# A decoder layer on one core: keys rotated by a permutation, low-rank products in two row slots, and a newly planned order

## The chip, the cores and the metric

The kernel runs on one core of a Trainium2 chip. A core has five engines with queues of their own: TensorE (PE in the profile; PEld is its weight load) multiplies matrices into PSUM, VectorE (DVE), ScalarE (ACT) and GpSimd (POOL) work on elements, and SyncE (SP) issues the transfers between DRAM and the on-chip memory SBUF. Each queue runs its instructions in the order in which they were written; semaphores hold an instruction back until its inputs are there. The time is device microseconds of one execution, from launch to end.

## What is computed

The layer works on x of shape (2 batches, 512 tokens, 1024 features), in three steps, each of which adds its result to x.

```python
x = x + attn(layernorm(x))      # 32 heads of 32 in 8 groups; weights sign(w) times a scale per row
x = x + xattn(layernorm(x))     # 256-wide reads, 16 heads of 16 with rotary positions and a causal mask,
                                # a state update, a gated product with ctx, a second state update
x = x + ffn(layernorm(x))       # x @ kernel + bias + low-rank terms picked by gate, and shared ones
```

Two lines of it are what the change touches. In the second step the keys (and queries) are rotated by position:

```python
x1, x2 = (x[..., :half], x[..., half:])
return jnp.concatenate([x1 * cos - x2 * sin, x2 * cos + x1 * sin], axis=-1)
```

In the third step the term of rank 32 is added to the dense product: `delta_flat = einsum('bor,btr->bto', B_eff, Ax)` with `Ax = einsum('bri,bti->btr', A_eff, x)`; batch rows are taken in eight groups of 128 tokens, each with factors of its own.

## The kernel before, in words

Tokens lie in tiles of 128, four per batch. The stages carry names that appear in the profile's tile names. `proj0` and `proj1` make q, k and v of the first attention (activations split in three bf16 parts). `maxA` and `maxB` compute the scores of batch 0 and batch 1 once and reduce them to row maxima; `attA` and `attB` compute them again, exponentiate and multiply by v. `outA` and `outB` are the output projections, `factor` makes the low-rank factors. `stateA` and `stateB` read the state, project and rotate q and k of the second attention; `maxC`, `attC`, `maxD`, `attD` are its maxima and attention; `tailA` and `tailB` are the state updates and the gated product; `weights`, `denseA` and `denseB` are the last step.

**Maxima.** `peaks` (L550) walks over groups of four heads. Per query tile, `scores` (L200) issues four matmuls with 32 contracted rows, one in each of the four 32-row slots of the array, into two pairs of PSUM banks; `reduced` (L581) takes maxima of each pair on VectorE (two reductions of 128x1024). When a group is done, `turned` (L588) splits the negated maxima into three bf16 parts, transposes them on TensorE, and copies them to a `shift` row. In the attention three rows of `shift` times a constant of ones (`ones16`) are added to the scores by a small matmul, which subtracts the maximum.

**Attention.** `attend` (L614) goes over groups and four key tiles: score matmuls, exponentials on ScalarE, value matmuls; `added` (L661) adds up the probabilities on VectorE, `finished` (L669) sums them over partitions on TensorE, and the result is scaled and split into three bf16 parts, partly on GpSimd. `direct` with `SPARE` decides whether the last key tile is added on VectorE or summed by extra matmuls.

**Rotation.** `rotations` (L865) computes sines and cosines of all positions (small instructions on VectorE, two table functions on ScalarE); `rotation_table` (L950) spreads them. `state_inputs` (L1105) first reads and normalises the four tiles of a batch (`tile_of`), keeping two numbers per token in `norm` for the tails. Then it projects: `kind` 0 gives queries, 1 gives keys, 2 gives keys with the two halves of each head exchanged, from a third weight matrix `proj[2]`. `rotated` (L1143) multiplies each bank by its row of the table and, for kind 2, adds the product to the key.

**Dense step.** `dense` normalises and transposes a tile, makes its 32 ranks (`bank` with four partial sums, then a matmul with `eye` that adds them into the 32 rows of `slot`), and multiplies: for each half of 512 columns eight matmuls of 128x512 with the weights and one of 32 rows with the low-rank factor `be`. `factors_back` loads the factors from DRAM.

**What sets the order.** The instruction order is written by a planner in the kernel's own Python code, not by the program's nesting. Every stage is a generator, a job, that yields (engine, estimated time, ready time) before it emits instructions. `run` (L449) keeps a clock per engine and always advances the job whose next step can start earliest, plus the job's lag; the lags are the numbers in the job list in `build` and in `LAGS`. `clocked` slows PE steps in the plan when PE had little to do in windows of 3.41 us. `take` and `give` keep count of tiles and PSUM banks: there are two single banks (`bank`), three double ones (`pair`), eight `page`, eleven `row` and four `probs` buffers. All instructions are pinned to the planned order on each engine, so estimates and lags decide the order, and the real waits decide the time.

Of the kernel before, what the change touches and what calls it, by code (L numbers as in the profile page):

```python
# [12 lines left out]
BF16 = mybir.dt.bfloat16  # L13
I32 = mybir.dt.int32
AF = mybir.ActivationFunctionType
ALU = mybir.AluOpType
# [53 lines left out]
class Kernel:  # L70
# [79 lines left out]
    def constants(self):  # L150
# [7 lines left out]
        self.ones16 = self.const([P, P], "ones16", BF16)  # L158
        nc.gpsimd.memset(self.ones16, 1.0)
# [19 lines left out]
        )  # L179
        self.eps = self.const([P, 1], "eps")  # L180
# [5 lines left out]
        )  # L186

# [234 lines left out]
    def output_weights(self):  # L422
# [7 lines left out]
        "added": 0.0, "ahead": 0.0, "attA.ahead": -0.1, "attA.exponentials": -0.1, "attA.finished": 0.3,  # L430
        "attB.added": 0.0, "attB.ahead": -0.3, "co.emptied": -0.1, "cv.emptied": -0.1, "denseA.summed": -0.6,
        "denseB.emptied": 0.3, "denseB.summed": -2.0, "emptied": -0.6, "exponentials": 0.3,
        "factor.put": -1.0, "finished": 0.0, "gained": -1.0, "gated": -1.0, "joined": -0.6, "k.scale_of": 0.0,
        "maxA.reduced": 0.0, "maxA.turned": -0.1, "maxB.reduced": 0.3, "maxB.turned": -0.3,
        "maxD.turned": -0.3, "outA.clean": 1.0, "outA.stored": 2.0, "outB.stored": -1.0,
        "proj0.featured": -1.0, "proj0.valued": -0.6, "proj1.featured": -1.0, "proj1.valued": -0.6,
        "q.scale_of": 0.0, "residual": 1.0, "rotated": 0.0, "stateA.emptied": -0.3, "stateA.rotated": -0.1,
        "stateB.gained": 0.0, "stateB.rotated": 0.0, "stored": 0.6, "summed": -0.6, "tableB.emptied": -2.0,
        "tailA.gained": -1.0, "tailA.residual": -2.0, "tailB.gated": -0.3, "tailB.residual": 0.0,
        "v.scale_of": 0.0, "wo.scale_of": 0.0,  # L440
    }
    SPARE = 3
# [145 lines left out]
    def turned(self, name, b, g, mx, reduced, earlier):  # L588
# [3 lines left out]
        t = yield "DVE", 1.2, t  # L592
# [3 lines left out]
        nc.vector.tensor_scalar(parts[:, :, :, 0], mx, -1.0, None, ALU.mult)  # L596
        nc.vector.scalar_tensor_tensor(rest, mx, -1.0, parts[:, :, :, 0], ALU.mult, ALU.subtract)
        nc.vector.tensor_copy(parts[:, :, :, 1], rest)
        nc.vector.tensor_tensor(parts[:, :, :, 2], rest, parts[:, :, :, 1], ALU.subtract)
# [14 lines left out]
    def attend(self, groups, operands, scale, causal):  # L614
# [10 lines left out]
        def exponentials(p, s, q0, t):  # L625
# [4 lines left out]
            if causal:  # L630

                done = yield "POOL", 1.0, done
                nc.gpsimd.affine_select(
                    out=p[:, :, q0 : q0 + P], in_=p[:, :, q0 : q0 + P], compare_op=ALU.is_ge, fill=0.0,
                    base=0, pattern=[[0, 4], [1, P]], channel_multiplier=-1,
                )
            return done

        def probabilities(g, kt):
# [10 lines left out]
            for j in range(4):  # L650
                r = slice(32 * j, 32 * j + 3)
                self.mm(
                    s[j // 2][:, j % 2, q0:], lhsT=self.ones16[r, :], rhs=shift[r, q0:], start=False, stop=True
# [110 lines left out]
    def attend_1(self, b, peaks):  # L764
# [6 lines left out]
        def operands(g):  # L771
# [8 lines left out]
            def dst(av, inv, t):  # L780
# [4 lines left out]
                t = yield "POOL", 1.2, t  # L785
# [6 lines left out]
                t = yield "POOL", 1.6, t  # L792
                nc.gpsimd.tensor_copy(d[1], rest)
                t = yield "POOL", 1.9, t
# [199 lines left out]

    def read(self, x, t, w, gb, nout, dst, wide):
# [59 lines left out]
        t = yield "DVE", 0.42 * nout, t  # L1055
        for o in range(nout):
            nc.vector.tensor_scalar(
                rows[o], rows[o], mv[:, o, 0:1], rstd[:, o : o + 1], ALU.subtract, ALU.mult
            )
# [30 lines left out]
    def state_weights(self):  # L1090
# [7 lines left out]
        self.proj = [w[0][:, 0], w[0][:, 1], w[1][:, 0]]  # L1098
        self.values = w[1][:, 1].rearrange("p a b -> p (a b)")[:, :512].rearrange("p (a b) -> p a b", a=2)
        for kind in range(3):  # L1100
# [4 lines left out]
    def state_inputs(self, b, wide):  # L1105
# [10 lines left out]
        def tile_of(q):  # L1116
# [5 lines left out]
            t = yield "DVE", 1.3, t  # L1122
            nc.vector.tensor_scalar(x, x, mv[:, 0, 0:1], r, ALU.subtract, ALU.mult)
            keep = self.small([P, 2], "norm", bufs=8)
            nc.vector.tensor_copy(keep[:, 1:2], r)
            nc.vector.tensor_scalar(keep[:, 0:1], mv[:, 0, 0:1], r, -1.0, ALU.mult, ALU.mult)
# [14 lines left out]
        firsts = {}  # L1141

        def rotated(bank, kind, g, dst, t):  # L1143
            if dst is None:
# [671 lines left out]
```

## Time and profile before

| what | value |
|---|---|
| median of three runs | 1138.42 us (1137.93 to 1139.0) |
| the profiled execution's own time | 1135.51 us |
| its span, first to last instruction | 1133.8 us |
| mean granted clock of TensorE | 0.965 |
| busy PE, DVE, ACT, POOL | 1063.1, 841.2, 442.8, 239.2 us |
| moved by DMA | 70.51 MB, mean 62 GB/s |

The span lies between the first and last instruction; the execution's own time includes what lies around it. In a profile line of the timeline the first number is the start in us from the span's beginning, the second the duration, then engine, code line, operation, output and inputs, and the count; in square brackets stands the idle time of that engine before it, with what ended it. In a line of groups the numbers after the first bar are the busy time of all and the mean nanoseconds of one, after the second bar the idle time. Line numbers are mostly those of helpers (L130 is the helper for matmuls, L133 that for transposes, L51 that for the pinned engine calls), so tile names tell more. A float32 matmul with 512 columns shows as two records.

The stages follow each other so: projections and maxima A to about 215 us, attA to 302, maxB with outA and factor to 431, attB to 535, outB with stateA to 612, maxC with stateB and attC to 725, maxD, attD and tailA to 870, tails and dense tiles to the end.

### The profile page before, as it was taken

What the parts mean: (1) busy time and instruction counts of PE and PEld (TensorE: products, weight loads), DVE (VectorE), ACT (ScalarE), POOL (GpSimd) and SP (SyncE); (2) the same over time, 40 slices, a digit from 0 to 9 for tenths busy, and PEclk for the clock granted to TensorE, in tenths of its full rate; (3) what the DMA queues carried; (4) which work ended last, traced back from release to release, by engine and by line L of the source; (5) the groups of instructions that cost most, each with busy time, mean ns of one, the idle gap of its engine ahead of it and who ended that gap; (6) DMA issues with size and microseconds to landing.
All of it is one profiled execution on the core that took longest, in us unless ns stands there. A gap on an engine that the chain in (4) does not pass through costs nothing.

```text
span 1133.8 us, 16121 instructions
## 1 busy us (share of the span) xinstructions
PE 1063.1 (94%) x6364; PEld 521.5 (46%) x6364; DVE 841.2 (74%) x1390; ACT 442.8 (39%) x711; POOL 239.2 (21%) x249
## 2 busy tenths in 40 slices
PE   4889999999999998999999899989988899999998
PEld 3554353333233632332555543545465465665643
DVE  7978888578878865887777961599668677788572
ACT  6762101388500215786221255224743232332310
POOL 3442333322222303454451012001200000000000
PEclk9999999999998997999999889979998999999999
DMA  6621000101214221240113000410151001011110
GB/s 256 203 82 28 20 10 20 29 20 29 61 33 177 95 64 39 61 168 1 38 56 116 8 11 16 172 38 1 57 197 68 33 20 55 11 48 38 38 37 38
DMA packets 24784, 70.51 MB, mean 62 GB/s; under 512 B 5234, under 2 KB 5252, under 8 KB 23684
## 3 DMA queue, kind: packets, MB, share of 16 engines
q1 hardware_dynamic: 24708, 69.48, 17.9%
q8 instruction: 50, 0.82, 0.3%
q14 instruction: 26, 0.21, 0.1%
HBM read 50.59 MB, written 10.49 MB: 54 GB/s over the span
## 4 chain that ended last, share of the span: by engine, by line
PE 79%; DVE 11%; ACT 5%; issue 2%; DMA 1%; POOL 1%; SPq 0%; ACTq 0%; DVEq 0%; POOLq 0%
PE proj_bank L130 8%; PE denseA_pair L130 6%; PE denseB_pair L130 6%; PE attA_pair L130 4%; PE outA_bank L130 4%; PE attB_pair L130 4%; PE tailB_bank L130 3%; PE attB_bank L130 3%; PE attA_bank L130 3%; PE maxB_pair L130 3%; PE maxA_pair L130 3%; PE tailA_bank L130 3%; PE outB_bank L130 3%; PE stateB_bank L130 3%; PE tailB_pair L130 3%; PE tailA_pair L130 3%
## 5 line engine op out<-in xcount | busy, mean ns | idle before, releaser
L51 DVE TENSOR_REDUCE maxB_mx<-maxB_pair 128x2 f32<-128x1024 f32 x64 | 75.3, 1217 | 21.7 <-PE maxB_pair L130 21.3
L51 DVE TENSOR_REDUCE maxA_mx<-maxA_pair 128x2 f32<-128x1024 f32 x64 | 75.5, 1216 | 14.0 <-PE maxA_pair L130 14.0
L130 PEld LDWEIGHTS <-start_slab 128*128 128x128 bf16 x480 | 44.7, 98 | 68.8 <-issue 21.1
L51 DVE TENSOR_TENSOR attB_probs<-attB_probs,attB_probs 128x1024 f32<-128x1024 f32 x46 | 62.6, 1401 | 13.8 <-PE attB_bank L130 13.5
L51 ACT ACTIVATE attB_probs<-attB_pair 128x1024 f32<-128x1024 f32 x64 | 62.6, 1023 | 20.9 <-PE attB_pair L130 10.8
L51 DVE TENSOR_TENSOR attA_probs<-attA_probs,attA_probs 128x1024 f32<-128x1024 f32 x46 | 56.6, 1282 | 16.9 <-PE attA_bank L130 8.5
L51 ACT ACTIVATE attA_probs<-attA_pair 128x1024 f32<-128x1024 f32 x64 | 62.1, 1021 | 9.7 <-PE attA_pair L130 9.4
L130 PE MATMUL proj_bank<-in_slab,start_slab 128*128 128x512 bf16 x240 | 55.5, 379 | 1.7 <-ACT in_slab L51 1.7
L130 PE MATMUL proj_bank<-in_probs,start_slab 128*128 128x512 bf16 x240 | 54.7, 380 | 0.0
L130 PE MATMUL maxB_pair<-maxB_row,proj_slab 32*128 32x512 f32 x256 | 47.4, 687 | 3.1 <-DVE maxB_mx L51 3.1
L51 POOL TENSOR_SCALAR proj_row<-proj_row 128x512 f32<-128x512 f32 x24 | 47.7, 1987 | 1.9
L130 PE MATMUL outA_bank<-wo_slab,attA_slab 128*128 128x512 bf16 x192 | 46.7, 392 | 0.7 <-ACT maxB_shift L51 0.7
L130 PE MATMUL attB_pair<-proj_slab,attB_row 32*128 32x512 f32 x256 | 46.7, 685 | 0.0
L51 ACT ACTIVATE proj_row<-proj_bank,cs 128x512 f32<-128x512 f32 x20 | 13.7, 686 | 80.8 <-PE proj_bank L130 60.2
L130 PE MATMUL outB_bank<-wo_slab,attB_slab 128*128 128x512 bf16 x192 | 43.3, 379 | 0.3 <-POOL attB_slab L51 0.3
L130 PE MATMUL attA_pair<-proj_slab,attA_row 32*128 32x512 f32 x256 | 41.6, 639 | 0.3 <-ACT attA_probs L51 0.3
L51 POOL MEMSET tailB_row<- 9x128 f32 x8 | 1.6, 195 | 186.4 <-PE tailB_bank L133 70.7
L130 PE MATMUL attB_bank<-attB_probs,proj_slab 128*32 128x512 f32 x256 | 38.4, 633 | 1.1 <-DVE tableA_slab L51 0.7
L51 ACT COPY maxB_shift<-maxB_bank 128x512 bf16<-128x512 bf16 x8 | 4.7, 586 | 84.7 <-PE maxB_bank L133 84.7
L51 POOL TENSOR_SCALAR proj_slab<-proj_row 128x512 f32<-128x512 f32 x24 | 14.9, 621 | 106.6 <-ACT proj_row L51 89.0
L130 PE MATMUL maxA_pair<-maxA_row,proj_slab 32*128 32x512 f32 x256 | 36.8, 640 | 0.0
L51 POOL TENSOR_SCALAR_AFFINE_SELECT attD_probs<-attD_probs 128x512 f32<-128x512 f32 x16 | 12.1, 754 | 113.8 <-ACT attD_probs L51 104.3
(410 smaller groups left out, 2321.8 us busy)
## 6 DMA issues: line engine op xcount, KB each, us to landing
in_page<-in_x_dram SPq DMA_DIRECT2D x8, 512.0 KB, 4.1
q_page<-in_q_weight_dram SPq DMA_DIRECT2D x8, 512.0 KB, 5.3
wo_page<-in_o_weight_dram SPq DMA_DIRECT2D x8, 512.0 KB, 3.4
tailW_slab<-in_write_dram SPq DMA_DIRECT2D x3, 752.0 KB, 7.1
maxA_row<-proj_slab SPq DMA_DIRECT2D x32, 64.0 KB, 2.0
attA_row<-proj_slab SPq DMA_DIRECT2D x32, 64.0 KB, 2.0
maxB_row<-proj_slab SPq DMA_DIRECT2D x32, 64.0 KB, 2.0
outA_page<-in_x_dram SPq DMA_DIRECT2D x4, 512.0 KB, 3.7
```

The costliest lines, as they stand in the source:

```text
L51: return self.kernel.pin(getattr(self.engine, name)(*args, **kw))
L130: self.pin(self.nc.tensor.matmul(*args, **kw))
```

## The change

In `state_inputs` the third projection goes. Keys are projected first: `keyed` copies the raw bank to a row on ScalarE, multiplies the bank by the cosine row of the table, multiplies the raw row by a constant permutation matrix `swap` on TensorE, multiplies that product by the sine row and adds. Queries come after the keys. One transfer of weights fewer is issued.

In `dense` the low-rank products of both column halves stand together behind all sixteen weight matmuls. The ranks are spread by `eyes`, 64 columns wide, into two neighbouring row slots; the factor of the second half is loaded into the neighbouring slot (five transfers instead of two large ones' second), so the two products use different row slots.

`turned` splits the plain maxima, and `minus16` holds -1 where `ones16` held 1. The two `norm` instructions move from VectorE to GpSimd. Estimates of some steps, many lags, needs and `SPARE` are different, and so the planned order is.

In the planned order of PE three places differ by more than a few instructions. The opening of `maxB` has seven score tiles before the first outA matmul, where there were four. Its closing has eighteen outA matmuls between the last score tile and the transposes of its maxima, and six more behind those, where there were none. At the end the last three dense tiles come after the last tail; the last two of them are interleaved, where there was one after the other and the last tail had one dense tile behind it in PE's queue before its own. On VectorE the arithmetic of `rotations` stands in `attA` behind the second group, where it was in the middle of `factor`.

```diff
-        self.ones16 = self.const([P, P], "ones16", BF16)
-        nc.gpsimd.memset(self.ones16, 1.0)
+        self.minus16 = self.const([P, P], "minus16", BF16)
+        nc.gpsimd.memset(self.minus16, -1.0)
+        self.swap = self.const([P, P], "swap")
+        halves = [t.rearrange("p (e h i) -> p e h i", h=2, i=8) for t in (self.swap, self.ident)]
+        for h in range(2):
+            nc.vector.tensor_copy(halves[0][:, :, h, :], halves[1][:, :, 1 - h, :])
+        self.eyes = self.const([P, 64], "eyes")
+        for h in range(2):
+            nc.vector.tensor_copy(self.eyes[:, 32 * h : 32 * h + 32], self.eye)
...
-    SPARE = 3
+    SPARE = 100
...
-        t = yield "DVE", 1.2, t
+        t = yield "DVE", 0.95, t
-        nc.vector.tensor_scalar(parts[:, :, :, 0], mx, -1.0, None, ALU.mult)
-        nc.vector.scalar_tensor_tensor(rest, mx, -1.0, parts[:, :, :, 0], ALU.mult, ALU.subtract)
+        e.tensor_copy(parts[:, :, :, 0], mx)
+        e.tensor_tensor(rest, mx, parts[:, :, :, 0], ALU.subtract)
...
-        self.proj = [w[0][:, 0], w[0][:, 1], w[1][:, 0]]
+        self.proj = [w[0][:, 0], w[0][:, 1]]
...
-            nc.vector.tensor_copy(keep[:, 1:2], r)
-            nc.vector.tensor_scalar(keep[:, 0:1], mv[:, 0, 0:1], r, -1.0, ALU.mult, ALU.mult)
+            yield "POOL", 0.4, t
+            nc.gpsimd.tensor_copy(keep[:, 1:2], r)
+            nc.gpsimd.tensor_scalar(keep[:, 0:1], mv[:, 0, 0:1], r, -1.0, ALU.mult, ALU.mult)
...
-            if dst is None:
-                t = yield "DVE", 0.69, t
-                nc.vector.tensor_tensor(kk[:, g, :], kk[:, g, :], to, ALU.add)
-                self.give("row", t)
...
+        def keyed(bank, g, t):
+            tr = max(t, (yield from self.take("row")))
+            tr = yield "ACT", 0.59, tr
+            raw = self.row([P, S])
+            nc.scalar.copy(raw, bank)
+            t = yield "DVE", 0.69, t
+            nc.vector.tensor_tensor(kk[:, g, :], bank, table[:, 1, :], ALU.mult)
+            self.give("bank", max(t, tr))
+            room = yield from self.take("bank")
+            tr = yield "PE", 0.97, max(tr, room)
+            other = self.bank([P, S])
+            self.mm(other, lhsT=self.swap, rhs=raw, start=True, stop=True)
+            t = yield "DVE", 1.38, max(t, tr)
+            nc.vector.tensor_tensor(raw, other, table[:, 2, :], ALU.mult)
+            self.give("bank", t)
+            nc.vector.tensor_tensor(kk[:, g, :], kk[:, g, :], raw, ALU.add)
...
-        for kind, (y, dst) in enumerate(((ys[0], qq), (ys[1], kk), (ys[1], None))):
+        for kind, y in ((1, ys[1]), (0, ys[0])):
...
+        for j in range(4):
+            t = yield from self.fetch(
+                self.be[32 * (j ^ 1) : 32 * (j ^ 1) + 32, :, 512:], src[32 * j : 32 * j + 32, :, 512:], 128, ready
+            )
...
-        slot = slice(32 * q, 32 * q + 32)
+        slots = [slice(32 * j, 32 * j + 32) for j in (q, q ^ 1)]
+        both = slice(64 * (q // 2), 64 * (q // 2) + 64)
...
-            self.mm(bank[slot, :], lhsT=self.eye, rhs=ax[:, 0, :], start=True, stop=True)
+            self.mm(bank[both, :], lhsT=self.eyes, rhs=ax[:, 0, :], start=True, stop=True)
...
-            if h == 0:
-                ready = max(t, (yield from self.join(ranks)))
-            t = yield "PE", 1.1, ready
-            self.mm(pair[:, h, :], lhsT=ax[slot, 1, :], rhs=self.be[slot, b, cols], start=False, stop=True)
+        t = yield "PE", 0.65, max(t, (yield from self.join(ranks)))
+        for h in range(2):
+            self.mm(
+                pair[:, h, :], lhsT=ax[slots[h], 1, :], rhs=self.be[slots[h], b, h * 512 : (h + 1) * 512],
+                start=False, stop=True,
+            )
...
-                ("rot", self.rotations(), 1.5, "attA.2"),
-                ("attA", self.attend_1(0, "maxA"), 0.0, "maxA.0"),
+                ("rot", self.rotations(), 1.0, "attA.2"),
+                ("attA", self.attend_1(0, "maxA"), 0.2, "proj1"),
...
-                ("attC", self.attend_2(0, "maxC"), 0.2, "maxC.0"),
+                ("attC", self.attend_2(0, "maxC"), 0.5, "maxC"),
```

Further hunks change estimates of steps (GpSimd steps of the attention from 1.0, 1.2, 1.6 and 1.9 to 0.75, 0.75, 1.0 and 1.35) and entries of `LAGS`.

## The prediction

> **What bounds the kernel now.** I read the page first: the busy row, the slices, and the shares of the chain of waits.
>
> ```profile
> PE 1063.1 (94%) x6364; PEld 521.5 (46%) x6364; DVE 841.2 (74%) x1390; ACT 442.8 (39%) x711; POOL 239.2 (21%) x249
> PE   4889999999999998999999899989988899999998
> PEclk9999999999998997999999889979998999999999
> PE 79%; DVE 11%; ACT 5%; issue 2%; DMA 1%; POOL 1%; SPq 0%; ACTq 0%; DVEq 0%; POOLq 0%
> ```
>
> TensorE (PE) is busy 1063.1 of 1133.8 us and is 79% of the chain, so a matmul taken out shortens the run unless VectorE (DVE) bounds that stretch. The dips in the clock row are the second thing to watch: a slowed matmul counts as busy too.
>
> The groups of matmuls, with shapes kept apart, price the two products that the change touches (a float32 matmul shows as two records, so x48 is 24 matmuls and x16 is eight):
>
> ```profile
> L130 PE MATMUL stateB_bank<-stateB_probs,stateW_slab 128*128 128x512 f32 x48 | 22.5, 605 | 0.0
> L130 PE MATMUL stateA_bank<-stateA_probs,stateW_slab 128*128 128x512 f32 x48 | 21.3, 596 | 1.1 <-ACT stateB_page L51 0.7 <-DVE stateA_slab L51 0.4
> L130 PE MATMUL denseB_pair<-factorsB_slab,denseB_row 32*128 32x512 f32 x16 | 9.0, 640 | 0.0
> L130 PE MATMUL denseA_pair<-factorsB_slab,denseA_row 32*128 32x512 f32 x16 | 8.9, 633 | 0.0
> ```
>
> The timeline shows what such products take when they follow one another: the last dense tile, a score tile of the second batch with output projection behind it, and the keys of the first batch.
>
> ```profile
> 419.50 1.14 PE L130 MATMUL maxB_pair<-maxB_row,proj_slab 32*128 32x512 f32 x8
> 420.57 2.76 PE L130 MATMUL outA_bank<-wo_slab,attA_slab 128*128 128x512 bf16 x12
> 599.00 12.28 PE L130 MATMUL stateA_bank<-stateA_probs,stateW_slab 128*128 128x512 f32 x28 [0.45 <-DVE stateA_slab L51]
> 1119.83 1.12 PE L130 MATMUL denseA_pair<-factorsB_slab,denseA_row 32*128 32x512 f32 x2
> 1120.88 7.13 PE L130 MATMUL denseA_pair<-weights_slab,denseA_page 128*128 128x512 f32 x16
> ```
>
> Fourteen full matmuls take 12.28 us, 0.88 each. One low-rank matmul alone takes 1.05 from its start to the next start (1119.83 to 1120.88); four matmuls of the same shape in four row slots take 1.07 together (419.50 to 420.57).
>
> Last, the stall between the maxima of batch 1 and its attention, as windows (PE, PEld, DVE, ACT, POOL busy, then granted clock) and in the timeline:
>
> ```profile
> 427.00:431.00 4.00, 0.72 (x8) 0.53 (x11) 3.86 (x8) 0.07 (x1) 0.00 (x0) 0.79 0.00 0
> 431.00:442.00 11.00, 11.00 (x48) 2.93 (x52) 3.52 (x4) 5.09 (x6) 8.62 (x16) 0.50 0.22 73
> 442.00:450.00 8.00, 8.00 (x68) 2.40 (x60) 6.69 (x6) 6.26 (x8) 0.00 (x0) 0.94 0.14 35
> ...
> 430.28 0.61 PE L133 MATMUL maxB_bank<-ident,parts 128*128 128x128 bf16 x4 [3.41 <-DVE parts L51]
> ```
>
> One pause of 3.41 us is followed by 11 us at half clock, with PE the bound: it costs 3.4 + 5.5 = 8.9 us.
>
> **The change, part by part.** The sum is made against the profiled execution (span 1133.8, its own time 1135.51); the median of the three runs, 1138.42, lies 2.9 above it, and I carry the differences over to the median.
>
> *Rotated keys.* Per batch the third projection goes: 4 groups x 2 matmuls. Four products with the constant `swap` come, of the same form. Net 4 matmuls of 0.88 per batch, 8 in all: -7.0 us. The vector work is the same, 12 instructions of 0.69 per batch for keys and queries. New are four copies of a bank on ScalarE (0.59 each, as the bank copies of attA), and ScalarE is busy only 1.9 of 21 us between 591 and 612. The chain of one key is longer (copy 0.6, product 0.9, multiply 0.7, add 0.7), and there are only two banks, so the danger is that PE waits for a bank. In the planned order of batch 0 the projection of the next group (1.75) lies between a projection and its swap product, longer than multiply or copy (0.7 each); followed by hand, one wait of half a microsecond stays, before the second query. Keys first, queries last, so the queries cover the last key. Ends: -7.0, and 0 if every one of the 8 swaps waits 0.9. I take -7.0: PE has no idle time in those 12.28 us and the cover is there in the order.
>
> *Low-rank products.* Per tile, two matmuls of 1.05 each at separate places become two in neighbouring row slots, into the two halves of a pair. The nearest row is four in four slots at 1.07, so I take 1.07 for the two: 1.03 saved per tile, 8 tiles, -8.3 us. Ends: 0 if the two do not overlap, -8.4 if they cost what one does. The spreading product with `eyes` has 64 output rows in place of 32 (0.38 us now, bounded by the 0.27 of a 128-wide transpose on one side and by 0.6 on the other: within +-2 us over 8, taken as 0). The ranks are needed 16 matmuls later instead of 8, which loosens a wait.
>
> *Small edits.* `swap` and `eyes`: four copies on DVE at the start, of 0.4 us or less by the copy of `spread` there, inside 2.85 us in which DVE waits for the first page. The maxima split without the sign: four instructions of 0.2 us as before. `norm` moves two instructions (0.15 and 0.20 us) per tile from DVE to POOL, eight times: at most 2.8 us of DVE, hidden by PE; behind them in POOL's queue stands the cleaning of outB, which waits if the statistics are late, but POOL is free half of the time there. One 512 KB load fewer with the state weights; the back-load of the second factor is five transfers instead of one, some 1.7 us more of SP's queue at about 0.4 us an issue, ahead of weights that land 14.4 us after issue; 0, at worst +2. The limit on direct sums (3 to 100) does nothing: 46 additions each in attA and attB is already the most that 8 groups give.
>
> *The order.* Most of the order is the same. Three places differ enough to price.
> (a) Closing of the batch-1 maxima. Before, the last score tiles stand together and PE waits for the last reduction. After, 18 outA matmuls (0.23 each, 4.1 us) stand between the last score tile and its transposes; the reductions (2.35) and the split (0.9) take 3.3. The pause goes, and with it the half clock: -8.9; ends -3.4 (clock falls for another reason) and -8.9.
> The Trainium skill ("TensorE: Matmul & The Clock Gate", Part 1) says that the clock returns to full after one busy window of about 3.4 us; as an estimate from that page the half clock would cost 1.7 us here and this term would be -5.1. The row shows 11 us at 0.50, so the row decides.
> (b) Opening of the same maxima, around 303 to 318. Before, outA starts at 309.9 after four score tiles; after, seven stand ahead of it in PE's queue. Three tiles are 3 x 2.35 us of reductions, plus a split (0.85) and one attA subtraction (0.7): outA starts 8.6 us later, of which PE fills 3 x 1.07 + 0.4 = 3.6. +5.0. The three tiles are not lost, the later bunch at 350 to 366 is one tile shorter; against that stands more half clock. Ends 0 and +10.
> (c) The 7 us of angle arithmetic (DVE, 383.7 to 390.7, hidden there: PE never pauses) now stand in attA. There a group takes 10.5 us and DVE works 8.85 of them, so the adds of one group come 7 - 1.7 = 5.3 us late; the sums that need them have 2 us of slack (adds end near 240.1, the sums start at 242.2). +3; ends 0 and +7.
> At the end the last tail is now covered by three dense tiles instead of one, and the 3 us between the last two tiles (1109.8 to 1112.8, transposes, ranks) lie beside another tile: -2; ends 0 and -3.
>
> Sum: -7.0 - 8.3 - 8.9 + 5 + 3 - 2 = -18.2. Against the median: 1138.4 - 18.2 = 1120.2, about 1120 us. What comes next where the stall of (a) is gone: attB at full clock, 97% of PE from there.
>
> **The rivals.**
> 1. *The pair does not overlap.* For it: no row shows two slots alone, and the records of the scores do not say how four share the time. Against: 1.07 for four leaves no room for serial work. It gives 1138.4 - 18.2 + 8.3 = 1128.5.
> 2. *The new order gives back what it wins.* (b) and (c) at their upper ends (+10, +7) and (a) at its lower (-3.4): -7.0 - 8.3 - 3.4 + 17 - 2 = -3.7, so 1134.7. For it: both places are bound by DVE, whose share is 72 of 99 us in attA and 12.6 of 13 between 297 and 310.
> 3. *Slower: the closing stage stalls on DVE.* The last tail write now has three dense tiles behind it, about 55 us of PE, so all eight tails' vector work must be done some 20 us earlier. Between 875 and 1094 DVE is busy 160 of 219 us; squeezed into 200 it is 80%, with PE in order behind it. The price is that of the pause at 427: 8.9 us each. From the third such pause on (26.7 against 18.2) the kernel is slower; three give 1147, the second leaves about even, 1138.
> 4. *More pauses vanish.* Windows at 0.7 of the clock also stand at 736 to 760 and 865 to 884, and two such pauses fewer give 1138.4 - 18.2 - 10 = about 1110. For it: less PE work moves every later window; against: the order there is nearly unchanged, and the maxima of batch 1 of the second attention are bound by DVE (22.2 of 24 us).
>
> **How the numbers follow.** Forecast, 1113 to 1126: 0.55. Rival 1 (1126 to 1132): 0.12. Rival 2 (1132 to 1136): 0.12. Rival 3 (over 1136): 0.10. Rival 4 (under 1113): 0.11. A measurement here tells about 0.2% (2.3 us) from no change. Of rival 3 the two-pause case (0.02) and of rival 2 its very end (0.01) are no change, 0.03; the rest of rival 3 is slower, 0.08; faster is what remains, 0.89. The range leaves out rival 3 and the lower half of rival 4: 1109 to 1135; it is wide because (b), (c) and the closing stage are priced by hand. The forecast's own range is 1113 to 1126.
>
> **What the profile after would show.** stateA_bank and stateB_bank with `stateW` as weights: x32 instead of x48, and x8 with `swap` in all four per batch at 0.88 each; ScalarE copies of 0.59 beside them. The low-rank rows start-to-next 1.07 for x4 records, not 2.1. No pause before the last maxB_bank and a clock near 1.00 from 430 on; outA starting about 318 with PE idle around it; attA some 3 us longer with the sums waiting for attA_probs. PE busy near 1043, idle still about 70. Wrong would make it: x4 records that take 2 us, PE waiting for DVE for over 3 us at a time after 875, or half clock at a place that has none now.

## The result and the profile after

The changed kernel takes 1151.68 us in the median (1148.56 to 1154.89) against 1138.18 beside it; the ratio on record is 1.0139, 95% interval 1.0116 to 1.0162 (the two medians alone divide to 1.0119). It is slower by 1.4%, where 1.6% faster was forecast. Run once more on another chip (`f3_after` below) it gave 1.0106, 1.0087 to 1.0126. The profiled execution took 1154.89 us, the longest of its four (span 1153.2, granted clock 0.943, against 0.965 before). All times below come from executions at a mean clock of 0.94 or more; the profiled execution of `f2_mid` ran at 0.556 and took 1701.07 us, so it and its trace are left out.

The page, busy row and slices:

```profile
PE 1068.6 (93%) x6316; PEld 529.7 (46%) x6348; DVE 840.1 (73%) x1380; ACT 446.5 (39%) x717; POOL 243.3 (21%) x265
PE   5889999989999999999999889999988899998998
PEclk9999999989978999999999689969998899998999
```

PE has 48 records fewer (the second profile of the same program has 6348, so 16 fewer are the change's and 32 are missing from this trace), and yet is busy 5.5 us longer; it is idle 84.6 us instead of 70.7. The clock row dips in places where it did not before. The groups of matmuls show that the operations themselves became cheaper, as planned:

```profile
L130 PE MATMUL stateB_bank<-stateB_probs,stateW_slab 128*128 128x512 f32 x32 | 15.8, 615 | 0.4 <-DVE stateB_slab L51 0.4
L130 PE MATMUL stateA_bank<-stateA_probs,stateW_slab 128*128 128x512 f32 x32 | 14.6, 599 | 0.0
L130 PE MATMUL stateB_bank<-stateB_row,swap 128*128 128x512 f32 x8 | 4.5, 644 | 1.7 <-DVE stateB_slab L51 1.6
L130 PE MATMUL stateA_bank<-stateA_row,swap 128*128 128x512 f32 x8 | 4.3, 618 | 0.7 <-DVE stateA_slab L51 0.7
L130 PE MATMUL denseA_pair<-factorsB_slab,denseA_row 32*128 32x512 f32 x16 | 4.9, 633 | 0.0
L130 PE MATMUL denseB_pair<-factorsB_slab,denseB_row 32*128 32x512 f32 x16 | 4.5, 640 | 0.0
```

The low-rank rows fell from 17.9 to 9.4 us, the projections with their swaps from 43.8 to 39.2. Against these 13 us saved stand slower matmuls and pauses. The timeline of PE shows the pauses (the number in brackets) where the kernel before had none, or shorter ones: 4.04 at the maxima of batch 0 of the second attention (1.26 before), 5.34 ahead of the first dense tile (2.82 before).

```profile
254.23 1.23 PE L130 MATMUL attA_pair<-proj_slab,attA_row 32*128 32x512 f32 x3 [3.65 <-ACT attA_probs L51]
664.78 0.58 PE L133 MATMUL maxC_bank<-ident,parts 128*128 128x128 bf16 x4 [4.04 <-ACT stateB_probs L51]
785.11 0.61 PE L133 MATMUL maxD_bank<-ident,parts 128*128 128x128 bf16 x4 [1.38 <-DVE parts L51]
832.65 0.92 PE L133 MATMUL tailA_bank<-ident,tailA_row 128*128 128x128 f32 x4 [1.35 <-DVE tailA_row L51]
864.36 0.38 PE L133 MATMUL tailA_bank<-ident,tailA_few 128*8 128x128 f32 x1 [2.52 <-ACT tailA_row L51]
894.28 1.11 PE L133 MATMUL denseA_bank<-ident,denseA_page 128*128 128x128 f32 x4 [5.34 <-DVE denseA_page L51]
```

Windows of the changed kernel (PE, PEld, DVE, ACT, POOL busy, then granted clock): attA; maxB with outA; attB; and the closing of the maxB maxima, where the kernel before paused and ran at 0.50.

```profile
216.30:312.60 96.30, 92.38 (x721) 28.67 (x720) 73.80 (x91) 74.98 (x87) 18.13 (x29) 0.95 0.13 34
312.60:441.40 128.80, 125.67 (x562) 52.10 (x568) 98.74 (x124) 13.58 (x22) 29.10 (x25) 0.89 0.23 78
441.40:539.50 98.10, 95.95 (x738) 30.19 (x738) 73.99 (x64) 76.50 (x92) 49.94 (x50) 1.00 0.25 83
...
431.00:442.00 11.00, 10.84 (x64) 4.55 (x68) 9.33 (x15) 0.59 (x1) 5.81 (x5) 1.00 0.01 2
```

The closing is as forecast: no pause, clock 1.00. The half clock stands elsewhere, in attA and at the opening of maxB.

The lengths of the stages, from the first and last products of each in the timelines (us), with two kernels of the experiments: "both, old order" (`e3_both`) has the new operations in the order of the kernel before.

| stretch | before | both, old order | changed | changed again |
|---|---|---|---|---|
| start to attA | 214.8 | 214.1 | 216.3 | 213.9 |
| attA to attB (with maxB, outA, factor) | 216.0 | 217.3 | 225.1 | 222.8 |
| attB | 102.7 | 102.1 | 98.1 | 98.0 |
| outB, states, maxC, attC | 190.7 | 189.2 | 193.4 | 192.5 |
| maxD to last product of attD | 118.6 | 119.2 | 127.6 | 126.1 |
| from there to the first dense product | 32.5 | 32.5 | 39.5 | 38.3 |
| from there to the end | 258.5 | 251.9 | 253.2 | 253.2 |

Between the second and the third column the order differs, and with it the engine (VectorE or ScalarE) that the plan picked for some thirty copies out of PSUM banks. The small edits (the split without the sign, `norm` on GpSimd) differ too. No run takes them apart from the order; in the second profile of the changed kernel no wait of PE for GpSimd between the end of attB and maxD is longer than 0.9 us (0.3 in the second column's). PE idles 77.2 us in the second column's profile and 84.6 and 86.0 in the two of the changed kernel; the rest of the 18 to 27 us is matmuls that take longer. Thirteen to fifteen of them lie in two rows that the prediction gave no price.

### The profile page after: what moved, and what is told of

Read it like the earlier page. It is cut to its first block, busy times and chain, and to the rows that moved or that the text cites. A ratio compares the mean times of both kernels' runs of the same rounds, so it can differ in the third digit from the quotient of the medians.

```text
span 1153.2 us, 16089 instructions
## 1 busy us (share of the span) xinstructions
PE 1068.6 (93%) x6316; PEld 529.7 (46%) x6348; DVE 840.1 (73%) x1380; ACT 446.5 (39%) x717; POOL 243.3 (21%) x265
## 5 line engine op out<-in xcount | busy, mean ns | idle before, releaser
L130 PE MATMUL maxB_pair<-maxB_row,proj_slab 32*128 32x512 f32 x256 | 52.2, 742 | 2.3 <-DVE maxB_mx L51 2.0
L130 PE MATMUL attA_pair<-proj_slab,attA_row 32*128 32x512 f32 x256 | 44.3, 666 | 3.9 <-ACT attA_probs L51 3.9
L130 PE MATMUL attB_pair<-proj_slab,attB_row 32*128 32x512 f32 x256 | 44.2, 639 | 0.4 <-ACT attB_probs L51 0.3
```

Source lines behind the costliest of these rows:

```text
L130: self.pin(self.nc.tensor.matmul(*args, **kw))
```

## The experiments

Two questions: do the operations do what they were priced at (theory A), and where does the order lose? To change the operations without the order, the planner's choice was replaced by a list of its own steps, written out; the changed kernel run from its list is the same program, instruction for instruction. This diff and those of the orders below are written in short; the kernels hold the lists themselves.

```diff
-                    if best is None or at + job.lag < best[0]:
-                        best = at + job.lag, at, job
+            job = there[order.pop(0)]      # order: (job, engine) of every step, as a planner chose it
```

**The low-rank pair alone, old order.** The hunks of `dense`, `factors_back` and `eyes` on the kernel before; the first of a tile's two low-rank steps leaves the list.

```diff
-            if h == 0:
-                ready = max(t, (yield from self.join(ranks)))
-            t = yield "PE", 1.1, ready
-            self.mm(pair[:, h, :], lhsT=ax[slot, 1, :], rhs=self.be[slot, b, cols], start=False, stop=True)
+        t = yield "PE", 0.65, max(t, (yield from self.join(ranks)))
+        for h in range(2):
+            self.mm(
+                pair[:, h, :], lhsT=ax[slots[h], 1, :], rhs=self.be[slots[h], b, h * 512 : (h + 1) * 512],
+                start=False, stop=True,
+            )
```

> The kernel before with the two low-rank products of a dense tile issued together in two row slots, after both halves, and the back-load that this needs; every other step stays where it was, in the order of the kernel before. Theory A (the operations do what they were priced at, and the loss lies in the order alone): the eight x2 records of denseA and denseB fall from 8.9 and 9.0 us to about 4.9 and 4.5 each, as in the changed kernel, and the time falls by 8 us, to about 1130. Rival B (the operations bring nothing on the path, since the tile waits at its end for the spread ranks or for the row slots): the rows fall, but PE stands idle as much longer, and the time stays within 2 us of 1138.

Measured: 1128.94 us, ratio 0.9933 (0.9919 to 0.9947), that is -7.6 us. Groups and one pair in the timeline:

```profile
L352 PE MATMUL denseA_pair<-factorsB_slab,denseA_row 32*128 32x512 f32 x16 | 4.5, 640 | 0.0
L352 PE MATMUL denseB_pair<-factorsB_slab,denseB_row 32*128 32x512 f32 x16 | 4.5, 640 | 0.0
...
1103.37 1.13 PE L352 MATMUL denseB_pair<-factorsB_slab,denseB_row 32*128 32x512 f32 x4
1104.43 1.09 PE L355 MATMUL denseA_bank<-ident,denseA_page 128*128 128x128 f32 x8
```

Two products in two row slots take 1.06 us to the next start, what one alone took. Theory A holds, rival B falls.

**The permuted keys alone, old order.**

```diff
-        for kind, (y, dst) in enumerate(((ys[0], qq), (ys[1], kk), (ys[1], None))):
+        for kind, y in enumerate(ys[:2]):
...
+            self.mm(other, lhsT=self.swap, rhs=raw, start=True, stop=True)
```

> The kernel before with the third projection of the rotated keys replaced by one product with the constant swap on a copy of the raw keys; the products stand where the third projection stood, everything else in the order of the kernel before. Theory A: 8 matmuls of 0.88 us fewer, less some waits of PE for the vector engine at the shorter products (0.7 and 1.7 us before the swap rows of the changed kernel): the time falls by 3 to 5 us, to about 1134. Rival B (the products with swap are bound by DVE, which has 1.4 us of work for each): nothing is gained, 1138, or a pause of over 2 us opens with half clock behind it, and the time is 1140 to 1145.

Here the swap products come behind all queries and keys, where the third projection stood. In the changed kernel the keys come first, and other products lie between a projection and its swap product.

Measured: 1134.28 us, ratio 0.9989 (0.9973 to 1.0005): -1.3 us, no more than the noise. The timeline of PE in the first batch:

```profile
605.24 1.03 PE L351 MATMUL stateA_bank<-stateA_row,swap 128*128 128x512 f32 x2
607.13 1.12 PE L351 MATMUL stateA_bank<-stateA_row,swap 128*128 128x512 f32 x2 [0.86 <-DVE stateA_slab L272]
608.87 1.10 PE L351 MATMUL stateA_bank<-stateA_row,swap 128*128 128x512 f32 x2 [0.61 <-DVE stateA_row L272]
610.10 0.66 PE L354 MATMUL stateB_bank<-ident,stateB_page 128*128 128x128 f32 x4
611.44 1.12 PE L351 MATMUL stateA_bank<-stateA_row,swap 128*128 128x512 f32 x2 [0.68 <-ACT stateB_page L272]
```

A product of 0.9 us follows a chain of 1.4 us on DVE, through two banks; PE waits between them until VectorE has emptied a bank. From the first projection to the values (590.79 to 614.16) it is 23.4 us against 24.0 before: of 3.5 us of matmul saved, 0.6 arrive. Rival B is nearer than A, without its pause of 2 us. That is the price in the old place; it is not shown for the changed kernel, whose rows above have 0.7 and 1.7 us of idle time before the swap products of the two batches.

**Both operations, old order.** The two edits above together.

> Both operations of the change, in the order of the kernel before. Theory A: the two gains add, 11 to 13 us, to about 1126; then the order of the changed kernel, which has the same operations and takes 1152, costs some 25 us. Rival B: the gains do not add to more than 4 us (1134 or more), and the operations carry a part of the loss. Between the two, around 1130, the shortened stages would have moved a stall.

Measured: 1128.46 us, 0.9927 (0.9911 to 0.9943), -8.3 us. It is the low-rank gain with little of the swap, 2.5 us short of the 1126 of theory A and 5.5 under rival B's bound. So the operations do not cost; the order of the changed kernel, with the same two operations and the small edits, costs 1.8 to 2.1% against this one (1.0106 and 1.0139 against 0.9927), 20 to 24 us.

**A filled pause.** To the kernel before:

```diff
+        if name == "maxB" and g == 7:
+            for _ in range(20):
+                self.turn_block(turns[:, 0, :], self.ident16, self.ident16)
```

> The kernel before with 20 transposes of a constant (0.15 us each, 3.1 us together), written into the bank that the last turned maxima of the batch-1 peaks use and overwritten by them, so that PE is busy during most of the 3.4 us in which it waited for the split maxima at 427. Their result is not used. Theory A (the pause is what brings the 11 us of half clock): the clock from 431 on is 1.00, and the time falls by 5.5 us, to about 1133. Rival C (the clock falls there for another reason, such as the stretch of bf16 and score products before it): the clock from 431 on is 0.5 as before and the time stays at 1138, or is a little above.

Measured: 1134.39 us, 0.9979 (0.9961 to 0.9998), -2.4 us. Timeline and windows:

```profile
428.84 1.29 PE L133 MATMUL maxB_bank<-ident 128*128 128x128 bf16 x20
432.32 0.40 PE L133 MATMUL maxB_bank<-ident,parts 128*128 128x128 bf16 x4 [2.19 <-DVE parts L51]
...
430.00:435.00 5.00, 2.66 (x21) 1.03 (x18) 4.39 (x10) 1.55 (x3) 1.26 (x2) 1.00 0.00 0
435.00:440.00 5.00, 4.88 (x39) 1.56 (x40) 2.05 (x2) 3.96 (x6) 4.31 (x3) 1.00 0.00 0
```

The transposes of a constant were quicker than planned (0.065 us each), so 2.19 us of pause stayed; but the clock is 1.00 behind it, and attB took 97.9 us in place of 102.7. So the pause brings the half clock, and rival C falls. Other traces agree: attB takes 101.4 to 102.7 us in the five kernels in which the pause of 3.41 stands ahead of it (before, `e1_rank`, `e2_swap`, `e3_both`, `e5_first`), 97.9 here and with a fuller fill (`e8_best`). In the time only half of the 4.8 us arrive, -2.4 +- 2.1; why was not shown.

**The angle arithmetic back in its old place**, everything else as in the changed kernel:

```diff
 attA/finished0 POOL
-rot DVE                         # 7 us of angle arithmetic
 attA/exponentials10 ACT
...
 maxB/reduced21 DVE
+rot DVE
```

> The changed kernel, step for step, but for the angle arithmetic: its 7 us of DVE work (with the sines on ACT and one last vector instruction) stand where the kernel before had them, among the factor products, and not in attA. Theory A (this one block on DVE is what makes PE wait 3.65 us in attA and run 10 us at half clock): attA ends near 303, as in the kernel before, and the time falls by 8 us, from 1152 to about 1144. Rival D (the time lost in attA is only moved: the stages behind it are bound by DVE too and lose as much again at the new place): attA is shorter by 8 us, but the time stays within 3 us of 1152.

Measured: 1151.1 us, ratio 1.0134 (1.0112 to 1.0155). The trace does what theory A said: no pause and clock 1.00 in attA, whose scores take 84.4 us instead of 90.9; 5.6 us are left of it at the start of attB. But this profile is the fastest of its five executions and the changed kernel's the slowest of its four; against the second profile of the changed kernel attB starts 0.9 us earlier. A part was only moved, as rival D said: attA's last score to attB takes 136.5 us here, 134.2 and 133.1 in the changed kernel's profiles. The ratio is that of the changed kernel to within 0.3%: of the 8 us expected nothing can be seen in the time.

**The old order up to attB, the new one behind.**

```diff
-order = new
+order = old[: old.index(("attB", "PE"))]
+order += [step for step in new if step not in order]
```

> The operations of the changed kernel; the steps up to the first score of attB in the order of the kernel before, all later ones in the order of the changed kernel. Neither new operation stands in the first part, so the two orders are compared there with equal work. By the traces attB starts 10.6 us earlier in the old order, and 4.6 of it come back as half clock after the pause at 427. Theory A (orders cost what the traces show): the time falls by 6 us, to about 1146. Rival D (what is won ahead is lost behind): 1150 to 1154. More than 9 us (below 1143) would say that the first part also sets a pause of the second.

Measured: 1147.42 us, 1.0113 (1.0095 to 1.0131): 0.3% under the first measurement of the changed kernel, 0.1% over the second. The whole first part is worth 0 to 3 us. Its profile still has the pause of 3.41 at 430 with attB at 101.5 us, and the later stretches keep the length of the changed kernel (126.1 and 38.3 us).

**The new order up to maxD, the old one behind.**

```diff
-order = new
+order = new[: new.index(("maxD", "PE"))]
+order += [step for step in old if step not in order]
```

> The operations of the changed kernel; its own order up to the first score of maxD, and from there the order of the kernel before, with the low-rank products as in the changed kernel. Theory A (the new order of maxD, the tails, attD and the dense tiles costs some 19 us: 14 of half clock and 4 of idle PE between 733 and 900, and more behind it): the time falls by 17 to 21 us, to about 1133. Rival E (the loss there follows from what the changed kernel has left undone before maxD, so that the old order behind it loses as well): 1145 or more.

Measured: 1137.27 us, 1.0025 (1.0011 to 1.0038): 9 to 13 us less than the changed kernel, where theory A said 17 to 21. maxD to the last product of attD takes 120.8 us, from there to the first dense product 32.6 (118.6 and 32.5 in the kernel before). Windows of these two stretches, first here, then in the changed kernel:

```profile
730.40:851.20 120.80, 110.44 (x824) 63.20 (x823) 90.51 (x183) 58.44 (x104) 12.74 (x20) 0.93 0.15 53
851.20:883.80 32.60, 25.16 (x170) 17.48 (x169) 27.52 (x47) 13.28 (x25) 0.20 (x1) 0.92 0.43 148
```

```profile
732.90:860.50 127.60, 117.94 (x824) 68.53 (x823) 90.35 (x182) 57.99 (x105) 11.97 (x20) 0.88 0.14 49
860.50:900.00 39.50, 28.71 (x171) 19.55 (x171) 29.42 (x49) 12.90 (x25) 0.20 (x1) 0.80 0.38 127
```

The matmuls are the same (824, and 170 or 171); they take 11 us longer at a clock of 0.88 and 0.80, and PE idles 2.6 us more. Rival E falls.

**The changed kernel again, and three beside it on the same chip.**

> The changed kernel once more, instruction for instruction, so that the three kernels beside it are compared with it on one chip. Ratio to the kernel before 1.012 to 1.016; a lone profile may differ by half clock at other places, so that its stages show which stalls come in every execution.

Measured: 1147.12 us, ratio 1.0106 (1.0087 to 1.0126), below the 1.012 to 1.016 expected. The profile has the same pauses to a hundredth of a microsecond (3.65 in attA, 1.37, 1.35, 2.52 and 5.34 behind the start of maxD; only the one at the maxC maxima is 5.61 here and 4.04 there), but not the same half clock. The windows behind the pause in attA, first here, then in the first profile:

```profile
252.00:258.00 6.00, 6.00 (x30) 1.44 (x30) 4.61 (x5) 2.68 (x3) 1.22 (x2) 0.51 0.09 23
258.00:264.00 6.00, 6.00 (x60) 1.81 (x56) 4.44 (x4) 5.06 (x7) 1.77 (x2) 1.00 0.22 55
```

```profile
252.00:258.00 6.00, 3.77 (x18) 0.87 (x18) 6.00 (x6) 3.16 (x4) 0.00 (x0) 0.55 0.01 3
258.00:264.00 6.00, 6.00 (x36) 1.54 (x36) 1.93 (x3) 2.77 (x4) 2.37 (x3) 0.60 0.18 44
```

A window's length times what its clock lacks to 1, doubled, gives the time at half clock: some 7 us here (with 1 us ahead of 252), some 10 us there.

**The angle arithmetic in five pieces.**

```diff
-        t = yield "DVE", 7.0, t
+        t = yield "DVE", 1.4, t         # and four more such steps between the parts
```

> The changed kernel with the angle arithmetic still in attA, but cut into five pieces of about 1.4 us, one behind every fourth addition of probabilities; DVE's work in attA is the same. Theory A (it is the block of 7 us that makes the additions late): no pause of PE in attA over 1.5 us, no half clock there, attA ends near 300 instead of 307, and the time falls by 5 to 8 us. Rival G (DVE's load in attA is too high with 7 us more, however cut): attA stays within 2 us of the changed kernel's length.

Measured: 1146.83 us, 1.0096 (1.0076 to 1.0117), 0.1% under the changed kernel beside it. In the trace theory A is right on place and cause: no pause over 1 us in attA, its scores end at 300.4, and at the end of attB (531.7) it stands where the kernel with the whole old first part stands (531.9). So it is the block and not DVE's load that stalls attA. But 3 us against the profile beside it are all that the trace shows, and 1 +- 3 the time: the expected 5 to 8 were missed.

**The old order from the end of attD.**

```diff
-order = new
+order = new[: last(new, ("attD", "PE")) + 1]
+order += [step for step in old if step not in order]
```

> The changed kernel in its own order up to the last product of attD, and from there in the order of the kernel before (the earlier repair from maxD on gave 13 us). Theory A (the pauses of 2.5 and 5.3 us before the first dense tile are made in this stretch, the rest of the 13 us in maxD and attD): the first dense product comes 6 to 7 us earlier, and the time falls by 5 to 8 us, to a ratio of about 1.008. Rival H (all of it lies here): 12 us or more, 1.003. Rival I (the stretch only inherits what attD leaves late): under 2 us, 1.012 or more.

Measured: 1139.21 us, 1.0031 (1.0014 to 1.0048): 0.75% (8.5 us) less than the changed kernel beside it. The two pauses are again 1.45 and 2.82:

```profile
858.92 0.27 PE L354 MATMUL tailA_bank<-ident,tailA_few 128*8 128x128 f32 x1 [1.45 <-ACT tailA_row L272]
...
882.98 1.11 PE L354 MATMUL denseA_bank<-ident,denseA_page 128*128 128x128 f32 x4 [2.82 <-DVE denseA_page L272]
```

The stretch takes 32.5 us, the one ahead of it 126.1 as in the changed kernel. Theory A in the trace (-6); in the time the 8.5 us lie between it and the 12 of rival H, whose ratio (1.003) was met because the changed kernel beside it came out at 1.0106. The ratio is within 0.06% of the kernel with the old order from maxD on (1.0025), less than either interval: that the 5 to 7 us by which maxD to attD is longer in the changed kernel's traces (127.6 and 126.1 against 120.8) are in the time too is not shown. In the changed kernel the stretch reads so on DVE:

```profile
887.93 2.35 DVE L51 TENSOR_TENSOR weights_slab<-weights_pair,weights_slab 128x1024 f32<-128x1024 f32 x2 [0.79 <-PE weights_pair L130]
890.21 1.28 DVE L51 BATCH_NORM_STATS2 denseA_st<-tailA_slab 128x6 f32<-128x512 f32 x2
...
892.54 0.96 DVE L51 TENSOR_TENSOR tailA_page<-tailA_row,tailA_g 128x768 f32<-128x768 f32 x1
893.42 0.81 DVE L51 TENSOR_SCALAR denseA_page<-tailA_slab,denseA_mv,denseA_rstd 128x1024 f32<-128x1024 f32 x1
```

In the kernel before, on DVE and PE:

```profile
865.35 2.35 DVE L51 TENSOR_TENSOR weights_slab<-weights_pair,weights_slab 128x1024 f32<-128x1024 f32 x2 [0.83 <-PE weights_pair L130]
866.82 1.10 PE L130 MATMUL tailA_bank<-read,tailA_page 128*128 128x64 f32 x8 [0.46 <-ACT tailA_row L51]
867.62 1.28 DVE L51 BATCH_NORM_STATS2 denseA_st<-tailA_slab 128x6 f32<-128x512 f32 x2
869.05 0.90 DVE L51 TENSOR_TENSOR tailA_page<-tailA_row 128x768 f32<-128x768 f32 x1
869.88 0.81 DVE L51 TENSOR_SCALAR denseA_page<-tailA_slab,denseA_mv,denseA_rstd 128x1024 f32<-128x1024 f32 x1
```

In both the statistics of the first dense tile stand behind the last addition of weights. In the changed kernel four instructions of a tail (1.8 us) stand between them and the normalised page, and PE has nothing left after 889; before, it was one instruction (0.90), and PE still had a product of the tail until 867.9.

**The old order up to maxD, the new one behind.**

```diff
-order = new
+order = old[: old.index(("maxD", "PE"))]
+order += [step for step in new if step not in order]
```

> Both operations; the order of the kernel before up to the first score of maxD, and the order of the changed kernel from there. Beside the earlier kernel that has the old order only up to attB (ratio 1.011) it differs in the order of outB, the state inputs, maxC and attC alone. Theory A (that middle stretch costs what the traces show, 4 us, and sets the pauses of no other): ratio about 1.007. Rival J (the middle costs 8 us or more, which is what is left of the order's 24 us when 13 behind maxD and 3 ahead of attB are taken off): 1.004 or less. Rival K (the middle costs nothing, what is left over is in the sum's uncertainty): 1.010 or more.

Measured: 1140.58 us, 1.0046 (1.0029 to 1.0062): 0.6% under the changed kernel beside it, 0.7% under the kernel with the old order up to attB alone. So outB to attC, with the small edits that this kernel lacks, cost 7 +- 3 us by the ratios; the table shows 3 to 4, with the pause at the maxC maxima (1.26 before, 4.04 and 5.61 in the changed kernel) in that stretch. Between theory A and rival J; the rest is open. The kernel with both operations in the old order (0.9927) differs from this one in the order from maxD on and in nothing else that is computed: that order costs 1.2%, 13 us.

**Two pauses filled, both operations, old order.** The fill above with 45 transposes, and ten of f32 ahead of the first dense tile's.

> Both operations in the order of the kernel before, and two of its pauses filled with transposes of a constant whose results are overwritten: 45 of bf16 (0.065 us each as measured, 2.9 us) ahead of the last turned maxima of batch 1 (pause 3.4), and 10 of f32 ahead of the transposes of the first dense tile (pause 2.8). Theory A (a pause costs its own length and, if it is long enough, the half clock behind it): no half clock at 431 and at 870, and 2 to 5 us less than with both operations alone, 1124 to 1126. Rival F (half clock comes in other executions at other places, so that two pauses filled change the median little): 1127 to 1129.

Measured: 1124.08 us (1123.17 to 1125.55), 0.9910 (0.9893 to 0.9928): faster than both kernels, by 0.9% and 2%, and lower than with both operations alone by 0.2%, within the two intervals. At 431 the clock is 1.00 and attB is 97.9 us long; from 867 on the clock fell all the same:

```profile
867.00:876.00 9.00, 7.65 (x32) 3.38 (x31) 8.76 (x20) 2.69 (x5) 0.20 (x1) 0.62 0.20 66
```

There a pause of 1.04 stayed between others of 0.46, 0.68 and 0.67; some short pauses close together went with half clock where the single 2.19 of the fill before did not.

## Why the prediction was wrong

The step that failed is "Most of the order is the same. Three places differ enough to price", and in rival 4 "the order there is nearly unchanged", said of 736 to 760 and 865 to 884. The order differed in many more places: on PE the two step lists part at some thirty points between outB and the end of attC and at a dozen more up to the first dense tile, so the three places named ahead of the prediction were not all. Two stretches without a price, maxD to attD and the last tails ahead of the first dense tile, carry 13 to 15 us in the traces. In the time the order from maxD on costs 9 to 13 us, of which 8.5 are shown by `f1_tail` for what stands behind attD. The stretch from outB to attC, 7 +- 3 us, had no price either.

One such place, read from the traces alone: in the old order a context product of the tails (3.81 us) stands on each side of the last turn of maxD, and covers the split of the maxima; in the new one both (8.80 in the profile, at half clock in part) stand behind it, and PE waits 1.38. Timeline of both operations in the old order, then of the changed kernel:

```profile
772.84 3.81 PE L351 MATMUL tailA_pair<-tailA_row,tailW_probs 128*128 128x128 f32 x32 [0.46 <-PE attD_pair L351]
776.49 0.39 PE L354 MATMUL maxD_bank<-ident,parts 128*128 128x128 bf16 x4
776.71 3.79 PE L351 MATMUL tailA_pair<-tailA_row,tailW_probs 128*128 128x128 f32 x32
```

```profile
785.51 8.80 PE L130 MATMUL tailA_pair<-tailA_row,tailW_probs 128*128 128x128 f32 x64
```

By terms:

- *Low-rank products*, -8.3 (8 times 1.03 is 8.2): measured -7.6. Right; rival 1 is out.
- *Rotated keys*, -7.0: measured -1.3, but in the old place, with the swap products last; there the chain is longer and needs a bank twice, and PE waits. In the changed kernel, keys first, the waits before the swap products are 0.7 us in batch 0, near the half a microsecond that the prediction kept, and 1.7 in batch 1, which it did not count. By those rows some 4.6 us of the 7.0 should arrive; no run shows it in the time.
- *(a) closing of maxB*, -8.9: the pause and its half clock went, as forecast, but the sum was wrong. attB is 4.6 us shorter, and the pause is not won: the 24 outA matmuls that fill it were taken from the opening, so that attA's last score to attB takes 133 to 135 us in either order. (a) and (b) should have been one term.
- *(b) opening*, +5: outA starts 16 to 20 us later in the changed kernel, but 6 to 10 of these are the late end of attA. Counted from attA's last score it comes 22.3 to 22.9 us later instead of 12.7, close to the 8.6 more that were worked out. The half clock at the opening is there too; yet attA's last score to attB is as long as it was.
- *(c) angle arithmetic*, +3: the mechanism was right (late additions, late exponentials), the pause of 3.65 and its half clock made it 7 to 8.5 us of attA; of it 1 to 6 were left at the end of attB (by the kernel with the arithmetic back in its old place and the one with five pieces), and in the time 1 +- 3.
- *End of the kernel*, -2: the last stretch is 1.3 longer, not shorter, than in the old order.
- *Small edits*, 0: nothing in the traces speaks against it, but no run has them alone.

Together (a), (b) and (c) gave -0.9, and the runs give 0 to +3 for them. Even with the right price for every named term the forecast would have stayed between -6 and -9 (-7.6, -1.3 to -4.6, 1.5 in the middle of 0 to 3, and 1.3), and the kernel is 12 to 16 us slower. Of the rivals the third came nearest: a stage that stalls on DVE, with half clock behind each pause. But it looked for the stall behind 875 and among the last dense tiles, where the changed kernel lost 1 us; it came ahead of the first one. Two of the three signs named beforehand as fatal were there: a wait of over 3 us for DVE behind 875 (5.34), and half clock at places that had none (254, 835).

The Trainium skill ("TensorE: Matmul & The Clock Gate", Part 1) was weighed at (a): by an estimate from its rule of one busy window of about 3.4 us the half clock of 11 us would have cost 1.7. The traces with and without the pause show 3.5 to 4.8, so the row (5.5) was nearer by the traces; the time of the fill, -2.4 +- 2.1, does not decide. Half clock that lasted 7 us in one execution and 10 in another, behind the same pause, fits neither as a fixed price.

## What to carry to other kernels

When a planner writes the order anew, price the order as a whole: compare the two programs of the bounding engine stretch by stretch, not only where the diff or the eye falls, and put pauses that share filling work into one term. Separate operations from order first: the new operations run in the old order's list took 0.7% off, the new order (with the small edits) put 2% back on. And before a matmul saved is booked, follow its replacement through banks and copies, in the place where it will stand: with nothing between to cover its longer chain, the shorter product was paid in waits, and 1.3 of 7.0 us arrived.

## What the runs showed of the hardware

Most pauses of PE came back to a hundredth of a microsecond in another execution of the same program; the half clock behind them did not. A pause of 3.65 us went with 7 us of it in one execution and 10 in another, one of 2.19 with none. The same program's time tends to follow the mean clock: the twelve executions with the permuted keys alone went from 1132.1 us at 0.967 to 1138.5 at 0.961 (correlation -0.93), and 23 of the kernel before on the same chip have -0.67. One profile therefore tells where PE waits, but the price of a half clock in it is one draw of several.

In the fill a bf16 transpose of a constant came every 0.065 us (20 in 1.29). The 0.15 expected was a quarter of the 0.61 that four turned maxima took at 430 in the kernel before, which is a duration and no spacing: the four shown in the old order's maxD took 0.39, with 0.22 from their start to the next.
